# A vision tower's linear attention: half of the last softmax moved into the last round, and the order of the work after it

## The chip, the cores and the metric

The kernel runs on one core of a Trainium2 chip. The core has five engines with a queue of instructions each, which are worked off in order: TensorE (PE in the profile; its weight loads are listed as PEld), VectorE (DVE), ScalarE (ACT), GpSimd (POOL) and SyncE (SP), which here issues most of the DMA transfers. The metric is device time in microseconds. Before the change three runs took 2774.36, 2775.22 and 2785.34 us; their median is 2775.22 us.

## What is computed

A batch of 128 images goes through a tokenizer and two transformer layers. The stream `h` holds 128 images x 64 tokens x 256 features. The change lies in the attention of layer 1, and in the first steps of the routing of the layer's experts that follows:

```python
def _to_heads(y, R, C, H, hd):
    y = y.reshape(R, C, H, hd).transpose(0, 2, 1, 3)
    return jnp.transpose(y, (2, 1, 0, 3)).reshape(1, H, C, R * hd)

q = _to_heads(x @ Wq.T + bq, R, C, H, hd)      # R = 128 images, C = 64 tokens, H = 8 heads
k = _to_heads(x @ Wk.T + bk, R, C, H, hd)
v = _to_heads(x @ Wv.T + bv, R, C, H, hd)
q = jax.nn.softmax(q, axis=-1)                  # over images and head features
k = jax.nn.softmax(k, axis=-2)                  # over the tokens of a head
q = q * float(q.shape[-1]) ** 0.5
context = jnp.einsum('bhnd,bhne->bhde', k, v)
out = jnp.einsum('bhnd,bhde->hbne', q, context)
# h = h + out, and then
logits = layernorm(h) @ gate_w + gate_b         # routing: 8 experts
idx = jnp.argmax(softmax(logits), axis=-1)      # each token goes to one expert
```

The head of a row is not a slice of the features here: the reshape cuts each image's 64 x 256 block so that eight neighbouring tokens form one head. Multiplying k by q first gives a small matrix of 64 x 64 scores for a head, and its product with v gives the output.

## The kernel before

**Rounds.** `linear_attention` (L1084 to L1436) goes through four rounds `n`, each for 16 tokens, that is, for two heads ("halves" `hh` 0 and 1). In a round, step `i` of 16 projects one token: `queries_keys` (L1179) multiplies it with the weights of q and k in TensorE, and `queries_keys_kept` (L1184) adds the bias in DVE and writes the result to the buffer `qk`. Step `i` fills column block `i` of 8 of the 128 columns (`t g`), so that half 0 is whole after steps 0 to 7, and half 1 after steps 8 to 15. `prepare` (L1390) does the layer norm and transposes of the tokens that come next.

**The softmax of a round lies in the following round.** The dictionary `work`, filled by `at(n, i, ...)` (L1351), says which steps go behind the projection `i` of round `n`. For the heads of round `n` these are, in round `n + 1`:

- `largest` (L1215, DVE), `maximum` (L1225: a transpose on TensorE, a reduction and a diagonal matrix on DVE), `spread` (L1233: a matmul that broadcasts the maxima), `q_less` (L1237, DVE) and `q_exp` (L1241, ACT): the exponential of q
- `k_max` (L1246, DVE), `k_less` (L1251, POOL), `k_exp` (L1255, ACT), `k_sum` (L1259, DVE), `k_over_sum` (L1263, POOL, for the last half of the last heads DVE): the softmax of k
- `values` (L1190: TensorE, copied by ACT) in the heads' own round, and `values_transposed` (L1204: TensorE, then four ACT instructions with the bias)
- `scores` (L1270): 64 matmuls, each as two passes in the trace, that alternate between the halves; `scores_kept` and `scores_sums` (L1279, L1283) normalise them; `mixed` (L1290, TensorE) multiplies with the values, `added` (L1301, DVE) adds to the stripe of 64 features of the stream, and `written` (L1307, SP) issues the stripe's two writes, to `hx` for the experts and to `out`.

**The stripe after it.** In round `n + 2` the finished stripe is transposed (`transposed`, L1315: TensorE, copied by ACT), multiplied with the gate weights (`gates`, L1328, TensorE; `gates_added`, L1340, DVE), and its partial row statistics are taken (`moments`, L1311, DVE).

The loop runs over `range(6)`: rounds 4 and 5 have no projections. Round 4 holds the values and the whole softmax of the last heads along with the gates of the heads before, and round 5 the gates and moments of the last stripe. The order of the instructions is written out by hand (`manual_schedule`): each engine's queue follows the order of the calls.

**Buffers that tie the steps together.** Two buffers for `qk`, two for the stripe `h`, one each for `v`, `vT`, `m`, `mc`, `dg`, `ks` and `am`; PSUM pools of three (`pp`: projections, values), two (`pt`: transposes), one (`ps`: maximum, broadcast, scores) and two buffers (`po`: products, gates).

**The routing.** `route` (L1495) is called next. Its tiles take the memory that the attention's pools give back. It first makes mean and reciprocal root of each row from the partial statistics `sth` (L1518 to L1527), then transposes the gate sums `lgs` (L1533), subtracts, and scales with `rs` (L1539 to L1540).

Of the kernel before, what the change touches and what calls it, by code (L numbers as in the profile page):

```python
# [11 lines left out]
F32 = mybir.dt.float32  # L12
# [7 lines left out]
P = 128  # L20
# [1063 lines left out]
def linear_attention(c, hd, hx, out, lgs, sth, wqk, bqk, wv, bv, wgb):  # L1084
# [4 lines left out]
    tc, nc = c.tc, c.nc  # L1089
    NG = 4  # L1090
    with (
# [70 lines left out]
        class Heads:  # L1162
# [9 lines left out]
            def load(self):  # L1172
                self.h = hp.tile([P, T, 64], F32, tag="h", name="h", bufs=2)
                nc.sync.dma_start(self.h, hd[:, :, self.n * 64 : self.n * 64 + 64])
# [49 lines left out]

            def maximum(self):  # L1225
# [37 lines left out]
            def k_over_sum(self, hh, n):  # L1263
                eng = nc.vector if self.n == 3 and hh == 1 else nc.gpsimd
                x = self.k[:, 16 * n : 16 * n + 16, hh * 64 : hh * 64 + 64]
                eng.tensor_mul(x, x, bcast(self.ks[:, hh, 16 * n : 16 * n + 16], 2, 64))
# [3 lines left out]
            def scores(self):  # L1270
                self.pa = pss.tile([P, 64], F32, tag="ps", name="pa")
                for d in range(32):
                    for hh in range(2):
                        r = slice(hh * 64, hh * 64 + 64)
                        nc.tensor.matmul(
                            self.pa[r, :], self.k[:, d, r], self.q[:, d, r], start=(d == 0), stop=(d == 31)
                        )
# [73 lines left out]
        def at(n, i, f, *a):  # L1351
            work.setdefault((n, i), []).append(lambda: f(*a))

        for n, x in enumerate(heads):
# [17 lines left out]
            for k, i in enumerate((0, 0, 1, 1, 2, 3, 4, 5)):  # L1372
                at(m, i + (4 if n == 3 else 0), x.values_transposed, k)
            at(m, 10, x.scores)
            at(m, 10, x.scores_kept)
# [4 lines left out]
            at(m, 15, x.written)  # L1380

            for k in range(8):
                at(m + 1, 1 + k, x.transposed, k)
            for k in range(4):
                at(m + 1, 8 + k, x.moments, 16 * k, 16)
            for k in range(2):
                at(m + 1, 4 + 4 * k, x.gates, k)
                at(m + 1, 5 + 4 * k, x.gates_added, k)

# [15 lines left out]
        with tc.manual_schedule():  # L1405
# [11 lines left out]
            for n in range(6):  # L1417
                x = heads[n] if n < 4 else None
                if x:
                    x.begin()  # L1420
                for i in range(16):
                    if x:
                        x.queries_keys(i)
                        prepare(4 * n + i // NG, i % NG)
                        if i == 8:
                            x.load()
                    for step in work.pop((n, i), ()):
                        step()
                    if x:
                        x.queries_keys_kept(i)  # L1430
                        if n < 3 and i in (6, 7, 8, 10, 11, 12, 14, 15):
                            x.values((6, 7, 8, 10, 11, 12, 14, 15).index(i))
                    elif n == 4 and i < 4:
                        heads[3].values(2 * i)
                        heads[3].values(2 * i + 1)
# [3 lines left out]
class Routing:  # L1439


    def __init__(self, c, gp, wg, bg):
# [36 lines left out]
        nc.vector.memset(self.one, 1.0)  # L1479

# [14 lines left out]
def route(c, k, gfd):  # L1495
# [5 lines left out]
    with (  # L1501
# [12 lines left out]
        mean, rs, var, m, gf, pos = (g1(n) for n in ("mean", "rs", "var", "m", "gf", "pos"))  # L1514


        parts = k.sth.rearrange("p t n (s k) -> p t (n s) k", k=3)
        nc.vector.tensor_reduce(mean, parts[:, :, :, 1], AX.X, ALU.add)  # L1518
        nc.vector.tensor_scalar_mul(mean, mean, 1.0 / 8)
        nc.vector.tensor_sub(dev, parts[:, :, :, 1], bcast(mean, 2, 8))  # L1520
        nc.vector.tensor_mul(sq, dev, dev)
        nc.vector.tensor_reduce(m, sq, AX.X, ALU.add)
        nc.vector.tensor_reduce(var, parts[:, :, :, 2], AX.X, ALU.add)
        nc.vector.tensor_scalar(m, m, 1.0 / 8, LN_EPS, ALU.mult, ALU.add)
        nc.vector.tensor_scalar_mul(var, var, 1.0 / D)
        nc.vector.tensor_add(var, var, m)
        inverse_root(c, var, rs, m)  # L1527
# [273 lines left out]
def vit_tower(ctx: ExitStack, tc: tile.TileContext, a, out):  # L1801
# [16 lines left out]
    with tc.tile_pool(name="gate", bufs=1) as gp:  # L1818
        k = Routing(c, gp, a["wg"], a["bg"])
        linear_attention(c, hd, hx, out, k.lgs, k.sth, a["wqk1"], a["bqk1"], a["wv1"], a["bv1"], a["wg"])  # L1820
        experts(c, hx, gfd, out, a["we1"], a["we2"], a["be2"], lambda: route(c, k, gfd))
# [68 lines left out]
```

## Time and profile before

| what | us |
|---|---|
| median of three runs | 2775.22 |
| profiled execution | 2783.14 |
| its span | 2781.3 |
| PE busy in the span | 2609.6 |
| DVE busy in the span | 2036.5 |
| linear attention, first projection | 1962.9 |
| last projection kept (L1186 ends) | 2214.92 |
| scores of the last heads normalised (L1288 ends) | 2257.84 |
| last stripe added (L1305 ends) | 2271.86 |
| first statistic of the routing (L1518) starts | 2292.94 |
| `rs` first used (L1540) starts | 2301.53 |

The lower rows are moments after the start of the span, read from the timeline. A timeline line has the start, the duration, the engine, the line of the code, the operation, output and inputs, the number of instructions merged, and in brackets how long the engine had been idle and what ended that. "PEclk" or granted clock is the share of its full clock that TensorE was given. A line in the table of windows has a stretch of time and its length, and then, for PE, PEld, DVE, ACT and POOL, the busy time and the number of instructions.

### The profile page before, as it was taken

What the parts mean: (1) busy time and instruction counts of PE and PEld (TensorE: products, weight loads), DVE (VectorE), ACT (ScalarE), POOL (GpSimd) and SP (SyncE); (2) the same over time, 40 slices, a digit from 0 to 9 for tenths busy, and PEclk for the clock granted to TensorE, in tenths of its full rate; (3) what the DMA queues carried; (4) which work ended last, traced back from release to release, by engine and by line L of the source; (5) the groups of instructions that cost most, each with busy time, mean ns of one, the idle gap of its engine ahead of it and who ended that gap; (6) DMA issues with size and microseconds to landing.
All of it is one profiled execution on the core that took longest, in us unless ns stands there. A gap on an engine that the chain in (4) does not pass through costs nothing. (4 is left out here: it accounts for less than half of the span.)

```text
span 2781.3 us, 76925 instructions
## 1 busy us (share of the span) xinstructions
PE 2609.6 (94%) x33260; PEld 1748.0 (63%) x33260; DVE 2036.5 (73%) x3017; ACT 1627.1 (59%) x3411; POOL 1628.1 (59%) x1389
## 2 busy tenths in 40 slices
PE   7989999999999998899999999998899965999997
PEld 3553444444444443688888888887466645888886
DVE  6759999999998997577777777776467755444443
ACT  3228889888888887466665666565354432233332
POOL 3329888888888887765566565643133211454444
PEclk9999999999999999899999999999899975999999
DMA  3000000000000000000000000000444433555554
GB/s 107 31 12 1 2 1 2 1 2 2 1 2 1 2 2 2 12 11 18 11 18 11 11 18 11 18 11 17 115 89 109 101 90 109 173 191 190 194 194 133
DMA packets 138063, 140.80 MB, mean 51 GB/s; under 512 B 107923, under 2 KB 121509, under 8 KB 130032
## 3 DMA queue, kind: packets, MB, share of 16 engines
q1 hardware_dynamic: 126816, 117.91, 14.2%
q0 software_dynamic: 7648, 14.77, 1.7%
q8 instruction: 263, 4.31, 0.6%
q10 hardware_dynamic: 3248, 3.09, 0.4%
q14 instruction: 88, 0.72, 0.1%
HBM read 103.93 MB, written 32.54 MB: 49 GB/s over the span
## 5 line engine op out<-in xcount | busy, mean ns | idle before, releaser
L495 POOL TENSOR_TENSOR m<-q,k 128x1024 f32<-128x1024 f32 x384 | 719.0, 1903 | 30.5 <-PE sc L297 16.1
L487 DVE TENSOR_TENSOR m<-pc,k 128x2048 f32<-128x2048 f32 (+1 forms) x320 | 646.7, 2058 | 0.5 <-ACT q L431 0.5
L297 PE MATMUL sc<-m,wide 128*32 128x512 f32 x4096 | 529.6, 598 | 12.0 <-DVE m L487 7.1
L496 ACT ACTIVATE m<-m 128x1024 f32<-128x1024 f32 x384 | 402.2, 1049 | 5.9 <-POOL m L495 5.2
L297 PEld LDWEIGHTS sc<-m,wide 128*32 128x32 f32 x4096 | 126.4, 109 | 259.7 <-issue 146.2
L505 ACT ACTIVATE m<-k,q 128x64 f32<-128x64 f32 x1024 | 270.9, 339 | 0.8 <-DVE k L378 0.8
L946 DVE TENSOR_REDUCE mx<-sc 128x16 f32<-128x1024 f32 x128 | 156.1, 1220 | 154.7 <-PE sc L934 131.9
L961 POOL TENSOR_TENSOR e<-e,mx 128x1024 f32<-128x1024 f32 x128 | 243.4, 1902 | 10.1 <-POOL mx L960 0.2
L906 ACT COPY qk<-pqk 128x512 f32<-128x512 f32 x256 | 139.0, 605 | 134.3 <-PE pqk L902 134.3
L960 POOL TENSOR_TENSOR mx<-mx,gate 128x16 f32<-128x16 f32 x128 | 27.6, 216 | 316.9 <-ACT z L991 153.2
L1724 PE MATMUL ph<-xt,w1s 128*128 128x256 f32 x896 | 203.3, 386 | 3.4 <-DVE xt L1715 3.0
L1740 PE MATMUL po<-w2s,hT 128*128 128x256 f32 x896 | 198.0, 379 | 0.0
L973 ACT COPY pT<-pt 128x512 f32<-128x512 f32 x256 | 138.8, 600 | 98.9 <-PE pt L970 98.1
L1724 PEld LDWEIGHTS ph<-xt,w1s 128*128 128x128 f32 x896 | 173.3, 194 | 29.2 <-DVE xt L1715 3.8
L1740 PEld LDWEIGHTS po<-w2s,hT 128*128 128x128 f32 x896 | 168.1, 190 | 21.7
L902 PE MATMUL pqk<-xT,w 64*128 64x128 f32 x2048 | 169.5, 289 | 2.7 <-issue 2.7
L947 DVE TENSOR_TENSOR e<-sc,mx 128x1024 f32<-128x1024 f32 x128 | 156.8, 1225 | 4.4
L1728 ACT ACTIVATE hT<-ph,w1s 128x256 f32<-128x256 f32 x224 | 93.3, 470 | 106.6 <-PE ph L1724 106.6
L1758 POOL DMA_INDIRECT out<-y,rout x56 | 56.7, 1013 | 168.6 <-ACT hT L1728 125.1
L953 DVE TENSOR_REDUCE mx<-e 128x16 f32<-128x1024 f32 x128 | 153.3, 1198 | 2.5 <-ACT e L950 2.4
L902 PEld LDWEIGHTS pqk<-xT,w 64*128 64x128 f32 x2048 | 142.3, 189 | 20.4 <-issue 11.1
L970 PE MATMUL pt<-ident,e 128*128 128x128 f32 x1024 | 142.9, 280 | 5.0 <-POOL e L961 1.5
(290 smaller groups left out, 4986.7 us busy)
## 6 DMA issues: line engine op xcount, KB each, us to landing
w1s<-in_we SPq DMA_DIRECT2D x30, 1028.0 KB, 5.3
w2s<-in_we SPq DMA_DIRECT2D x30, 1024.0 KB, 5.0
hd<-h SPq DMA_DIRECT2D x16, 512.0 KB, 3.2
x<-hd SPq DMA_DIRECT2D x16, 512.0 KB, 3.9
h<-hd SPq DMA_DIRECT2D x4, 2048.0 KB, 12.7
hx<-h SPq DMA_DIRECT2D x4, 2048.0 KB, 11.4
out<-h SPq DMA_DIRECT2D x4, 2048.0 KB, 20.6
xt<-in_x SPq DMA_DIRECT2D x15, 512.0 KB, 3.5
```

Source lines behind the costliest of these rows:

```text
L297: nc.tensor.matmul(dst[j : j + 32], wide[:, hf, s : s + 32], part, start=start, stop=stop)
L487: nc.vector.tensor_tensor(m, bcast(self.pq[:, hf, i : i + n], 3, T), k, ALU.max)
L495: nc.gpsimd.tensor_tensor(m, bcast(self.q[:, hf, s : s + 2], 3, T), k, ALU.subtract)
L496: nc.scalar.activation(m, m, AF.Relu)
L505: nc.scalar.activation(self.parts[i, hf][:, q], self.blk.k[:, hf, i], AF.Relu, bias=self.q[:, hf, i - NB // 2, q : q + 1], scale=-1.0,)
L902: nc.tensor.matmul(pq[par][:, k, eh, :], w[r, f : f + P], self.xT[r, fc], start=True, stop=True)
L946: nc.vector.tensor_reduce(mx, sc, AX.X, ALU.max)
L947: nc.vector.tensor_sub(e, sc, bcast(mx, 2, T))
L953: nc.vector.tensor_reduce(self.sm[x], self.e[x], AX.X, ALU.add)
L961: nc.gpsimd.tensor_mul(e, e, bcast(sm, 2, T))
L1724: nc.tensor.matmul(ph[:, j], self.w1[:, w0 : w0 + P], self.xt[:, fc], start=(fc == 0), stop=(fc == 1))
L1740: nc.tensor.matmul(po, self.hT[:, f, r * P : r * P + P], self.w2[:, f, :], start=(f == 0), stop=(f == 7))
```

## The change

- The softmax of the last heads is split by halves. Half 0, whole after step 7 of round 3, goes into steps 9 to 15 of round 3 (`largest_of`, `maximum_of`, `spread_of`, `q_less_of`, `q_exp_of`, `k_exp_of`, and the old steps of k for half 0). Half 1 follows the last projection.
- Rounds 4 and 5 are replaced by `last`, which writes out one order: softmax of half 1 between the eight `values`; `scores` of half 0 and, after the last values and two transposes, of half 1; the sums; products and additions; the writes; and after these the transposes, gates and moments of the stripes of heads 2 and 3.
- Three of the four groups of moments of heads 1 go from round 3 to `last`, as fillings between the steps of heads 3.
- The stripe of heads 3 lies in a `qk` buffer instead of an `h` buffer, and its load is issued in step 11 of round 3.
- The row statistics go from `route` to a method `statistics` of `Routing`, called in `last`, with the attention's own tiles as scratch. `mean` and `rs` become tiles of the pool that outlives the attention.

```diff
             def load(self):
-                self.h = hp.tile([P, T, 64], F32, tag="h", name="h", bufs=2)
+                if self.n == 3:
+                    h = hp.tile([P, 2, 32, P], F32, tag="qk", name="h3", bufs=2)
+                    self.h = h[:, 0].rearrange("p d n -> p (d n)").rearrange("p (t f) -> p t f", f=64)
+                else:
+                    self.h = hp.tile([P, T, 64], F32, tag="h", name="h", bufs=2)
                 nc.sync.dma_start(self.h, hd[:, :, self.n * 64 : self.n * 64 + 64])
...
+            def largest_of(self, hh):
+                r = slice(hh * 64, hh * 64 + 64)
+                if hh == 0:
+                    self.m = hp.tile([P, 8, P], F32, tag="m", name="m")
+                m = self.m.rearrange("p s n -> p (s n)")[:, hh * 512 : hh * 512 + 512]
+                self.mh = m = m.rearrange("p (s n) -> p s n", n=64)
+                nc.vector.tensor_max(m, self.q[:, 0:8, r], self.q[:, 8:16, r])
+                for s in (16, 24):
+                    nc.vector.tensor_max(m, m, self.q[:, s : s + 8, r])
+                for s in (4, 2, 1):
+                    nc.vector.tensor_max(m[:, 0:s], m[:, 0:s], m[:, s : 2 * s])
+
+            def maximum_of(self, hh):
+                pool, tag = (pss, "ps") if hh else (pst, "pt")
+                pm = pool.tile([64, P], F32, tag=tag, name="pm")
+                nc.tensor.transpose(pm, self.mh[:, 0, :], c.ident)
+                self.mc = hp.tile([P, 1], F32, tag="mc", name="mc")
+                self.dg = hp.tile([P, P], F32, tag="dg", name="dg")
+                nc.vector.tensor_reduce(self.mc[0:64], pm, AX.X, ALU.max)
+                nc.vector.tensor_scalar_mul(self.dg[0:64, 0:64], c.ident[0:64, 0:64], self.mc[0:64])
+
+            def spread_of(self, hh):
+                pool, tag = (pss, "ps") if hh else (pst, "pt")
+                self.pb = pool.tile([P, 64], F32, tag=tag, name="pb")
+                nc.tensor.matmul(self.pb, ones[0:64], self.dg[0:64, 0:64], start=True, stop=True)
+
+            def q_less_of(self, hh, n):
+                x = self.q[:, 16 * n : 16 * n + 16, hh * 64 : hh * 64 + 64]
+                nc.vector.tensor_sub(x, x, bcast(self.pb, 1, 16))
...
-            def scores(self):
-                self.pa = pss.tile([P, 64], F32, tag="ps", name="pa")
+            def scores(self, heads=(0, 1)):
+                if 0 in heads:
+                    self.pa = pss.tile([P, 64], F32, tag="ps", name="pa")
                 for d in range(32):
-                    for hh in range(2):
+                    for hh in heads:
...
-        for n, x in enumerate(heads):
+        for n, x in enumerate(heads[:3]):
...
             at(m, 10, x.scores)
+            if m == 3:
+                at(m, 10, heads[3].k_max, 0)
             at(m, 10, x.scores_kept)
...
             at(m, 15, x.written)
+            if n == 2:
+                continue
 
             for k in range(8):
                 at(m + 1, 1 + k, x.transposed, k)
-            for k in range(4):
+            for k in range(4 if n == 0 else 1):
                 at(m + 1, 8 + k, x.moments, 16 * k, 16)
...
+        x = heads[3]
+        at(3, 9, x.largest_of, 0)
+        at(3, 11, x.load)
+        at(3, 11, x.maximum_of, 0)
+        at(3, 12, x.spread_of, 0)
+        for i in range(2):
+            at(3, 11, x.k_less, 0, i)
+            at(3, 12 + i, x.q_less_of, 0, i)
+            at(3, 13, x.k_exp_of, 0, i)
+            at(3, 14, x.q_exp_of, 0, i)
+            at(3, 15, x.k_over_sum, 0, i)
+        at(3, 14, x.k_sum, 0)
+
+        def last():
+            x, y, z = heads[3], heads[2], heads[1]
+            x.k_max(1)
+            x.values(0)
+            x.k_less(1, 0)
+            x.k_less(1, 1)
+            x.largest_of(1)
+            x.values(1)
+            x.values(2)
+            x.k_exp_of(1, 0)
+            x.maximum_of(1)
+            x.values(3)
+            x.k_exp_of(1, 1)
+            x.spread_of(1)
+            x.q_less_of(1, 0)
+            x.values(4)
+            x.q_exp_of(1, 0)
+            x.q_less_of(1, 1)
+            x.k_sum(1)
+            x.values(5)
+            x.q_exp_of(1, 1)
+            x.k_over_sum(1, 1)
+            x.k_over_sum(1, 0)
+            x.values(6)
+            x.scores((0,))
+            x.values(7)
+            z.moments(16, 16)
+            for i in range(2):
+                x.values_transposed(i)
+            x.scores((1,))
+            x.scores_kept()
+            x.values_transposed(2)
+            x.scores_sums()
+            x.values_transposed(3)
+            z.moments(32, 16)
+            for i in range(4):
+                x.mixed(i)
+                for j in (4 + 2 * i, 5 + 2 * i):
+                    if j < 8:
+                        x.values_transposed(j)
+                (z if i == 0 else y).moments((48, 0, 16, 32)[i], 16)
+                x.added(i)
+            x.written()
+            for i in range(4):
+                y.transposed(i)
+            y.gates(0)
+            x.moments(0, 64)
+            for i in range(4, 8):
+                y.transposed(i)
+            y.gates_added(0)
+            y.gates(1)
+            y.moments(48, 16)
+            for i in range(4):
+                x.transposed(i)
+            y.gates_added(1)
+            t = gp.tile([P, NG, D], F32, tag="x", name="dev", bufs=4)
+            routing.statistics(t, gp.tile([P, NG, D], F32, tag="x", name="var", bufs=4))
+            x.gates(0)
+            x.gates_added(0)
+            for i in range(4, 8):
+                x.transposed(i)
+            x.gates(1)
+            x.gates_added(1)
...
-                eng = nc.vector if self.n == 3 and hh == 1 else nc.gpsimd
+                eng = nc.vector if (self.n, hh, n) == (3, 1, 0) else nc.gpsimd
```

`statistics` has the instructions that stood at L1518 to L1527, and `route` begins with the transposes of `lgs`.

More of the change, by code (lines that the diff above doesn't have):

```diff
@@ L1081, in expert_attention, with linear_attention @@
         assert not work
-def linear_attention(c, hd, hx, out, lgs, sth, wqk, bqk, wv, bv, wgb):
+def linear_attention(c, hd, hx, out, k, wqk, bqk, wv, bv, wgb):
     tc, nc = c.tc, c.nc
+    lgs, sth, routing = k.lgs, k.sth, k
     NG = 4
@@ L1223, in largest, with q_exp_of, k_exp_of @@
                         nc.vector.tensor_max(self.m[:, 0:s], self.m[:, 0:s], self.m[:, s : 2 * s])
+            def largest_of(self, hh):
[24 more added lines that the diff above has]
+                nc.vector.tensor_sub(x, x, bcast(self.pb, 1, 16))
+            def q_exp_of(self, hh, n):
+                x = self.q[:, 16 * n : 16 * n + 16, hh * 64 : hh * 64 + 64]
+                nc.scalar.activation(x, x, AF.Exp)
+            def k_exp_of(self, hh, n):
+                x = self.k[:, 16 * n : 16 * n + 16, hh * 64 : hh * 64 + 64]
+                nc.scalar.activation(x, x, AF.Exp)
             def maximum(self):
@@ L1372, in linear_attention @@
             for k, i in enumerate((0, 0, 1, 1, 2, 3, 4, 5)):
-                at(m, i + (4 if n == 3 else 0), x.values_transposed, k)
+                at(m, i, x.values_transposed, k)
             at(m, 10, x.scores)
+            if m == 3:
+                at(m, 10, heads[3].k_max, 0)
             at(m, 10, x.scores_kept)
@@ L1416, in linear_attention @@
             groups[4].load()
[L1417 to L1420, printed above, removed]
+            for n, x in enumerate(heads):
+                x.begin()
                 for i in range(16):
[L1422 to L1426, printed above, removed]
+                    x.queries_keys(i)
+                    prepare(4 * n + i // NG, i % NG)
+                    if n < 3 and i == 8:
+                        x.load()
                     for step in work.pop((n, i), ()):
                         step()
[L1429 to L1435, printed above, removed]
+                    x.queries_keys_kept(i)
+                    if n < 3 and i in (6, 7, 8, 10, 11, 12, 14, 15):
+                        x.values((6, 7, 8, 10, 11, 12, 14, 15).index(i))
+            last()
         assert not work
@@ L1479, in __init__, with statistics @@
         nc.vector.memset(self.one, 1.0)
+        self.c = c
+        self.mean, self.rs = (gp.tile([P, T], F32, name=n) for n in ("mean", "rs"))
+    def statistics(self, t, u):
+        nc, mean = self.c.nc, self.mean
+        dev, sq = (t[:, 2 * i : 2 * i + 2].rearrange("p a (t n) -> p (a t) n", n=8) for i in range(2))
+        var, m = (u[:, i, 0:T] for i in range(2))
+        parts = self.sth.rearrange("p t n (s k) -> p t (n s) k", k=3)
+        nc.vector.tensor_reduce(mean, parts[:, :, :, 1], AX.X, ALU.add)
+        nc.vector.tensor_scalar_mul(mean, mean, 1.0 / 8)
+        nc.vector.tensor_sub(dev, parts[:, :, :, 1], bcast(mean, 2, 8))
+        nc.vector.tensor_mul(sq, dev, dev)
+        nc.vector.tensor_reduce(m, sq, AX.X, ALU.add)
+        nc.vector.tensor_reduce(var, parts[:, :, :, 2], AX.X, ALU.add)
+        nc.vector.tensor_scalar(m, m, 1.0 / 8, LN_EPS, ALU.mult, ALU.add)
+        nc.vector.tensor_scalar_mul(var, var, 1.0 / D)
+        nc.vector.tensor_add(var, var, m)
+        inverse_root(self.c, var, self.rs, m)
 def inverse_root(c, x, y, t):
@@ L1513, in route @@
         pb, oh, cs, dev, sq = g8("pb"), g8("oh"), g8("cs"), g8("dev"), g8("sq")
[L1514 to L1527, printed above, removed]
+        m, gf, pos = (g1(n) for n in ("m", "gf", "pos"))
+        mean, rs = k.mean, k.rs
         pl = gpp.tile([P, 2, 4, 4, 32], F32, name="pl")
@@ L1819, in vit_tower @@
         k = Routing(c, gp, a["wg"], a["bg"])
-        linear_attention(c, hd, hx, out, k.lgs, k.sth, a["wqk1"], a["bqk1"], a["wv1"], a["bv1"], a["wg"])
+        linear_attention(c, hd, hx, out, k, a["wqk1"], a["bqk1"], a["wv1"], a["bv1"], a["wg"])
         experts(c, hx, gfd, out, a["we1"], a["we2"], a["be2"], lambda: route(c, k, gfd))
```

## The prediction

> **What bounds the kernel now.** I read the page first: TensorE is busy for 94% of the span, but the share is lowest, and the granted clock too, in slices 32 to 34, where the linear attention ends and the routing begins. The page's chain of waits names only the last instruction, so it decides nothing here. I then asked for the windows by stage, and last for the timeline from the last round to the routing, which gives the order.
>
> The windows; columns are busy time of PE, weight loads, DVE, ACT, POOL, then granted clock, DMA share, GB/s:
>
> ```profile
> 2151.00:2215.00 64.00, 58.59 (x440) 35.99 (x439) 46.60 (x118) 30.17 (x64) 16.62 (x12) 0.97 0.43 91
> 2215.00:2257.90 42.90, 33.14 (x276) 24.42 (x274) 32.22 (x89) 24.34 (x52) 11.24 (x6) 0.88 0.41 98
> 2257.90:2293.00 35.10, 23.43 (x184) 18.75 (x184) 14.60 (x75) 4.49 (x8) 0.00 (x0) 0.67 0.50 120
> 2293.00:2318.00 25.00, 0.99 (x4) 0.92 (x4) 23.09 (x71) 0.79 (x2) 0.00 (x0) 0.50 0.06 18
> ```
>
> The first row is round 3, bound by TensorE. In the next two, 78 us after the last projection, no engine is full: a chain runs through all of them. The timeline of that chain:
>
> ```profile
> 2190.92 3.95 PE L1275 MATMUL pa<-qk 128*64 128x64 f32 x128
> 2194.92 0.22 DVE L1281 COPY am<-pa 128x64 f32<-128x64 f32 x1 [2.89 <-PE pa L1275]
> ...
> 2198.74 2.00 PE L1297 MATMUL po<-am,vT 64*128 64x64 f32 x32 [0.91 <-DVE am L1288]
> ...
> 2200.77 1.28 DVE L1305 TENSOR_TENSOR h<-h,po 128x512 f32<-128x512 f32 x2 [1.49 <-PE po L1297]
> ...
> 2214.23 0.69 DVE L1186 TENSOR_TENSOR qk<-pq,bs 128x512 f32<-128x512 f32 x1 [0.64 <-PE pq L1182]
> ...
> 2257.61 0.23 DVE L1288 TENSOR_TENSOR am<-am,rq 128x64 f32<-128x64 f32 x1
> 2257.89 12.47 PEld L1297 LDWEIGHTS po<-am,vT 64*128 64x128 f32 x128 [2.45 <-DVE am L1288]
> 2257.89 12.66 PE L1297 MATMUL po<-am,vT 64*128 64x64 f32 x128 [2.31 <-DVE am L1288]
> ...
> 2270.57 1.29 DVE L1305 TENSOR_TENSOR h<-h,po 128x512 f32<-128x512 f32 x2 [2.13 <-PE po L1297]
> 2271.89 0.51 SPq L1309 DMA_DIRECT2D hx<-h  x1
> 2272.44 9.07 SPq L1309 DMA_DIRECT2D out<-h  x1
> ...
> 2292.94 0.83 DVE L1518 TENSOR_REDUCE mean<-sth 128x64 f32<-128x512 f32 x1 [6.00 <-DMA out<-h]
> ...
> 2301.53 0.69 DVE L1540 TENSOR_TENSOR pb<-pb,rs 128x512 f32<-128x512 f32 x1
> ```
>
> The reader is to see four stretches: last projection kept at 2214.92; 42.9 us of softmax until the scores are normalised (2257.84); 14.0 us of products and additions until 2271.86; 29.7 us until 2301.53. The last holds gates, moments and a DVE idle for 6.00 us on the write of the stream, which lands 21.0 us after its first issue, and only then the row statistics. From L1540 on the code is the same in both kernels.
>
> The granted clock in the third stretch:
>
> ```profile
> 2176.00:2180.00 4.00, 0.41 (x4) 0.17 (x2) 1.59 (x4) 4.00 (x4) 2.89 (x2) 1.00 0.00 0
> 2180.00:2184.00 4.00, 3.58 (x11) 2.17 (x12) 3.96 (x11) 2.91 (x5) 2.16 (x2) 0.60 0.02 4
> ...
> 2260.00:2264.00 4.00, 4.00 (x42) 4.00 (x40) 1.54 (x3) 0.00 (x0) 0.00 (x0) 0.50 0.02 4
> 2264.00:2268.00 4.00, 4.00 (x42) 4.00 (x40) 1.87 (x4) 0.00 (x0) 0.00 (x0) 0.50 0.00 0
> ```
>
> An idle of about 4 us costs the clock, and the 64-column products at full occupation don't bring it back: they take 12.66/4 = 3.17 us per quarter, against 2.00 us at 2198.74.
>
> **The change part by part.** I carry the new order forward on all queues with these durations and compare the same four points.
>
> *Round 3.* DVE loses three groups of moments (3 x 2.11 = 6.3 us) and gains the half maximum (3 x 0.69 + 0.43 + 0.29 + 0.2 = 3.0), a k maximum (2.27), a reduction and a diagonal (0.58), two subtractions (2 x 1.21), a sum and a reciprocal (2.64): 10.9 us. Not the sum but the waits count. Half maximum and k maximum fit where moments stood and where DVE idled for 2.89 us before L1281. But the transpose of the maximum stands on TensorE behind the first product (ends 2200.7), and DVE waits for it with the next kept projection and the additions queued behind: transpose 0.3, reduction and diagonal 0.6, kept projection 0.7, addition done 2203.7 instead of 2202.05. The next product starts on the addition's first half and ends 2205.1; the broadcast queued behind it (0.4) is what the first subtraction awaits: subtraction to 2206.7, kept projection 2207.4, addition 2208.7; product 2 to 2210.7; second subtraction and kept projection fit in that time; addition 2212.1, sum and reciprocal 2214.7, kept projection 2215.4, addition 2216.7, last kept projection 2217.4: **2.5 us later** than 2214.92. ACT (four exponentials of half an operand, about 1.05 each) and POOL (four multiplications or subtractions of 1.90) idle there: L1199 was preceded by 17.6 idle us on ACT, L1253 by 38.6 on POOL. The load of the last feature stripe now waits only for the scores of head pair 2 (2194.9; it was issued at 2197.83), ahead of that pair's writes on SP; it lands after some 12.7 us, over 30 us before use. Both cost nothing.
>
> *Softmax and scores.* DVE from 2217.4: k maximum 2.3, half maximum 3.1, to 2222.8; transpose, reduction, diagonal to 2223.8. TensorE does values 0 to 2 meanwhile, then value 3 (3.62/2 = 1.8 plus a small gap, 1.86) and the broadcast, to 2225.4. From there TensorE is the longest: values 4 to 6 to 2231.0. Beside it DVE subtracts twice, sums, inverts (2230.5) and multiplies one half while POOL takes the other (2232.4). Then scores of half 0, value 7 (1.86) and its copy (0.6), two transposes (1.1), scores of half 1, copy, sum matmul, reciprocal and product (1.7).
>
> The scores were 128 passes in 3.95 us, 31 ns each, the halves alternating between two column ranges. A projection pass streams 512 columns in about 0.43 us, 54 ns for 64, so neighbouring passes overlap. Split, nothing alternates. Bounds for 64 passes: 31 ns, 2.0 us; 30 ns weight load plus 54 ns stream with no overlap, 5.4 us. I take 54 ns, 3.5 us, since consecutive passes of the same range (the projections) overlap their weight loads.
>
> So: 2231.0 + 3.5 + 1.86 + 0.6 + 1.1 + 3.5 + 1.7 = 2243.3, **14.5 us earlier** than 2257.84.
>
> The Trainium skill, "TensorE: Matmul & The Clock Gate", Part 3, says that a weight load overlaps matmuls in flight only where the row group differs. Split halves use all rows, so by that rule alone each half would take the 5.4 us, and the gain below shrinks by 3.8 us; the trace before, whose halves also share all rows, shows 3.81 us of weight loads inside 3.95 us of passes, against it.
>
> *Products and additions.* Four value transposes moved in between make TensorE 4 x 3.17 + 4 x 1.07 = 17.0 us at the low clock, while DVE has five groups of moments and four additions, 5 x 2.1 + 4 x 1.3 = 15.7; that is the bound at full clock. From the normalised scores to the last addition I take 17.3 (the low clock arriving after the first product), bounds 15.7 and 18.8: 2260.6, **11.3 us earlier**.
>
> The same page, Part 1, has the full clock return after some 3.4 us of activity; the rows at 2260 to 2268 show 0.50 over fully busy windows and differ. By the page this stretch would be at 15.7 us and the gain 1.6 us more.
>
> *After the last addition.* DVE in order: moments of the stripe 64 x 0.13 = 8.3, gate addition 0.69, moments 2.1, gate addition 0.69, statistics 8.3 (the same instructions that stood between 2292.94 and 2301.53, now without the subtractions between them), two gate additions 1.4, product 0.7, eight subtractions with the wait for the last transpose 1.6: 23.8 us, to 2284.4. TensorE and ACT do sixteen stripe transposes and four gate matmuls beside it: 2277.43 to 2281.74 shows 4.3 us per quarter, 17.2 us and some start at the low clock; they end about 2281, with the statistics. The write lands at 2260.6 + 21.0 = 2281.6, the first product of the routing asks for it at 2282.1. Three things end within 1 us, so each earlier one is worthless, each later one costs.
>
> Sum: 2284.4 against 2301.53, **17.1 us less**. The routing and experts (from 2301.53 to the end) stay. The profiled execution took 2783.14 us (span 2781.3); it would take 2766.0. That execution lies 7.9 us above the median of the runs, 2775.22 (2774.36, 2775.22, 2785.34); from the median the forecast is 2758 us.
>
> **The rivals.**
> 1. Dear scores and an early low clock: split passes without overlap, and the clock falls at the first scores (about 2236) instead of in the products. For it: low-activity products didn't bring the clock back. Against: the scores at 2190.92 kept 1.00. At 84 ns a pass, 3.8 us are lost; with values, transposes and scores at the low clock some 5 more: gain 7 to 11 us, 2764 to 2768.
> 2. The write takes over: the wait that the page shows (6.00 us) stays, as the stripe's write now runs beside other DMA or is issued later. Against: the write rows agree (20.4 median, 21.0 most). Every microsecond beyond 0.5 counts; 5 us more gives 2763.
> 3. Slower: the waits added to round 3 let the clock fall there. One gap of over 3.5 us on TensorE between 2198 and 2217 does it, as at 2176. Then five steps of projection and product take 6.9 us instead of 3.85 (15 us), eight values 3.6 instead of 1.86 (14 us), scores 3: 32 us lost, 15 slower, 2790. Against: the largest gap that I find there is 1.4 us. It decides only from a gap of 3.5 us.
> 4. Cheap scores (2.0 each) and the full clock throughout: 17.1 + 3.0 + 1.6, gain near 21 us, 2754.
>
> **How the numbers follow.** Forecast 0.57, rival 1 0.20, rival 2 0.08, rival 3 0.06, rival 4 0.09. The likeliest case is 2758 with 2754 to 2763. The range takes rivals 1, 2 and 4, with some 3 us of scatter between runs: 2750 to 2771. A 0.5% step, 14 us, is about what these runs can tell from no change; it lies at 2761.3, inside the forecast's own range. Faster: most of the forecast (0.50) and rival 4 (0.09), a little of rival 2: 0.61. Slower: rival 3, 0.06. The rest is 0.33.
>
> **What would show it.** Right: last kept projection 2 to 3 us later than before relative to the round's start; half scores of 3 to 4 us each; normalised scores 26 us after the last kept projection (before: 42.9); last addition to the routing's first product about 21.5 us, with hardly a wait for the write. Wrong: a granted clock below 1.0 in round 3, a half score of 2.0 or 5.4 us, DVE idle on the write for several microseconds, or a routing and expert stage that itself changes its length.

## The result and the profile after

The changed kernel takes 2760.72 us (median of five runs, 2759.70 to 2765.45), the kernel before, run beside it, 2777.53 us. The ratio is 0.9931 with a 95% interval of 0.9917 to 0.9944: it is faster by 0.7%. Later comparisons of the unchanged pair gave 0.9931 (0.9914 to 0.9948) and 0.9947 (0.9926 to 0.9968). The profiled execution took 2759.7 us, its span is 2757.9 us.

Executions of both kernels fall into two groups some 8 us apart, which part in the tokenizer, long before the change (its last convolution matmul starts at 125 to 126 us or at 131 to 133 us), and the two profiles that are compared here belong to different groups; so stages are measured from the first projection of the linear attention.

The time by stage, in us. "Rounds" runs from the first projection to the last kept one, "softmax" to the normalised scores, "products" to the last addition, "after" to the first use of `rs`; "experts" goes from the end of the routing's last matmul to the end of the span:

| execution | rounds | softmax | products | after | sum of these | experts |
|---|---|---|---|---|---|---|
| before | 251.98 | 42.92 | 14.02 | 29.67 | 338.59 | 435.44 |
| after | 256.44 | 31.13 | 14.91 | 23.41 | 325.89 | 433.42 |
| after, forecast | 254.5 | 25.9 | 17.3 | 23.8 | 321.5 | 435.4 |

So the linear attention gives 12.7 us where 17.1 were forecast, and the experts, untouched, some 2 us more. The windows of the changed kernel by stage, with smaller windows where the clock matters (time, then busy time of PE, weight loads, DVE, ACT, POOL, then granted clock, DMA share, GB/s):

```profile
2141.30:2210.70 69.40, 63.12 (x446) 38.31 (x446) 51.11 (x84) 34.90 (x69) 24.16 (x16) 0.93 0.41 86
2210.70:2241.80 31.10, 25.84 (x210) 21.83 (x208) 18.06 (x34) 11.68 (x24) 7.46 (x3) 0.95 0.56 135
2241.80:2256.70 14.90, 14.60 (x176) 12.23 (x176) 14.90 (x89) 7.83 (x26) 0.00 (x0) 1.00 0.01 2
2256.70:2280.10 23.40, 12.28 (x75) 6.80 (x72) 21.87 (x117) 6.34 (x12) 0.00 (x0) 0.87 0.74 180
...
2192.00:2196.00 4.00, 4.00 (x20) 1.78 (x18) 2.22 (x5) 0.00 (x0) 0.00 (x0) 0.57 1.37 220
...
2204.00:2208.00 4.00, 4.00 (x36) 2.24 (x34) 2.79 (x3) 0.00 (x0) 1.60 (x1) 0.79 0.00 0
...
2216.00:2220.00 4.00, 0.70 (x3) 0.61 (x4) 3.41 (x5) 0.70 (x1) 1.66 (x1) 0.92 0.91 214
2220.00:2224.00 4.00, 4.00 (x13) 2.89 (x12) 0.85 (x3) 0.95 (x2) 0.00 (x0) 0.65 0.90 219
```

Three things are to be seen. The products stage, whose windows stood at 0.50 before, holds the full clock, and DVE is busy in all of it. The clock is lost earlier instead: in round 3 (0.57 and 0.79), and once in the softmax (0.65), behind a window in which TensorE worked for 0.70 us of 4. The timeline of the same stretches:

```profile
2189.63 2.00 PE L1344 MATMUL po<-am,vT 64*128 64x64 f32 x32 [0.91 <-DVE am L1335]
2191.57 0.30 PE L1248 MATMUL pm<-ident,m 128*64 128x128 f32 x1
2191.70 3.27 PE L1189 MATMUL pq<-w,xT 128*128 128x512 f32 x4
...
2202.57 3.52 PE L1189 MATMUL pq<-w,xT 128*128 128x512 f32 x4
...
2213.07 4.59 POOL L1299 TENSOR_TENSOR qk<-qk,ks 128x1024 f32<-128x1024 f32 x2 [2.91 <-DVE ks L1295]
...
2213.62 4.58 DVE L1241 TENSOR_TENSOR m<-m,qk 128x512 f32<-128x512 f32 x2
...
2219.30 0.40 PE L1248 MATMUL pm<-ident,m 128*64 128x128 f32 x1 [4.18 <-DVE m L1243]
...
2219.50 3.52 PE L1203 MATMUL pv<-wvs,xT 128*128 128x256 f32 x8
...
2222.94 0.43 PE L1257 MATMUL pb<-dg,ones 64*128 64x64 f32 x2
...
2228.68 3.94 PE L1322 MATMUL pa<-qk 128*64 128x64 f32 x64
...
2236.25 3.94 PE L1322 MATMUL pa<-qk 128*64 128x64 f32 x64
...
2256.73 0.51 SPq L1356 DMA_DIRECT2D hx<-h  x1
...
2277.99 0.69 DVE L1664 TENSOR_TENSOR dev<-wsum,mean 128x512 f32<-128x512 f32 x1 [0.57 <-DMA out<-h]
...
2280.12 0.69 DVE L1670 TENSOR_TENSOR pb<-pb,rs 128x512 f32<-128x512 f32 x1
```

A projection of four passes takes 3.27 and 3.52 us instead of 1.98. Two steps of the half maximum (L1241) take 4.58 us, 2.29 each, beside POOL's subtractions, which take as long. TensorE idles for 4.18 us before the transpose of the maximum, and the value behind it takes 3.52 us instead of 1.9. A half of the scores takes 3.94 us. The wait on the stream's write is 0.57 us, where it was 6.00.

### The profile page after: what moved, and what is told of

Read it like the earlier page. It is cut to its first block, busy times and chain, and to the rows that moved or that the text cites. A ratio compares the mean times of both kernels' runs of the same rounds, so it can differ in the third digit from the quotient of the medians.

```text
span 2757.9 us, 76947 instructions
## 1 busy us (share of the span) xinstructions
PE 2602.5 (94%) x33263; PEld 1744.7 (63%) x33263; DVE 2038.5 (74%) x3024; ACT 1628.9 (59%) x3415; POOL 1633.7 (59%) x1390
## 6 DMA issues: line engine op xcount, KB each, us to landing
h<-hd SPq DMA_DIRECT2D x4, 2048.0 KB, 12.8
out<-h SPq DMA_DIRECT2D x4, 2048.0 KB, 21.3
```

## The experiments

The theory: the gain of the softmax and of the stage after the last addition is real; the part that is missing is lost to a clash of DVE and POOL early in the softmax, to the clock that falls behind it, to the split of the scores, and in round 3 to added waits and clock falls. The rivals: the scatter between executions makes the difference; or the write, the place of the moments, or TensorE's order sets the end instead.

**The changed kernel again**, without an edit.

> The changed kernel once more, as the yardstick for the runs beside it. Between the first projection and the first use of rs the two profiles differ by 325.9 against 338.6 us, 12.7 us; the rest of the 23.4 us between the two spans lies before the attention (8.7) and in the experts (2.0). Theory A: only the 12.7 us, and perhaps 2 in the experts, belong to the change, and the 8.7 are scatter between executions: the median is then 2760 to 2766, and the first projection of this profile lies anywhere from 1954 to 1963. Theory B: the change also makes the stages ahead of it faster: the first projection lies at 1954 to 1955 again, and the median at 2757 to 2761.

Measured: 2760.05 us in the median (six runs), ratio 0.9931. The first projection comes at 1961.0 us, as it does before the change (1962.9), and the stages repeat: 255.85, 31.07, 14.90, 23.38, with 433.73 us of experts. Its span is 2764.2 us, 17.1 below that of before in the same group; the two profiles shown above differ by 23.4, of which 8.7 lie ahead of the attention. The scatter doesn't make the gain.

**The kernel before again.**

> The kernel before, unchanged, profiled a second time. Theory A (what the change does after the first projection is the same in every execution): linear attention from the first projection to the first use of the reciprocal root takes 338 to 339 us, with 64.6 us for round 3, 42.9 for the softmax and 29.6 after the last addition, whether the first projection comes at 1954 or at 1962 us. Routing's end to the end of the span takes 435.4 us again if the 1.7 to 2.0 us that the experts are shorter after the change belong to the change, and 433 to 434 if they are scatter. Theory B (the readings of before belong to its slower tokenizer): with a first projection at 1954 us the linear attention itself is several microseconds different.

Measured: 341.25 us for the linear attention (rounds 252.89, softmax 43.41, products 15.29, after 29.66), experts 434.96. The stages repeat within 1.3 us, and the experts stay at 435. Round 3 is 66.2 us instead of 64.6, and the timeline of this execution tells why:

```profile
2198.67 2.00 PE L1297 MATMUL po<-am,vT 64*128 64x64 f32 x32 [0.91 <-DVE am L1288]
2200.60 3.42 PE L1182 MATMUL pq<-w,xT 128*128 128x512 f32 x4
```

The clock falls once (0.70 in the window from 2202 us) in the kernel before too, with none of the new waits. The longest idle of TensorE nearby is 0.91 us, which the first execution of before has as well, without a fall. So a fall in round 3 is not brought by the change alone.

The first profile of before, against which 12.7 us were counted, had no such fall. Over the two profiles of before (338.59 and 341.25 us) and the three of the changed kernel (325.89, 325.20 and, in the last run below, 324.44) the linear attention gives 14.7 us on average and the experts 1.8. Together that is 16.6 us, about what the medians show (16.8).

**Statistics back in the routing.**

```diff
-            t = gp.tile([P, NG, D], F32, tag="x", name="dev", bufs=4)
-            routing.statistics(t, gp.tile([P, NG, D], F32, tag="x", name="var", bufs=4))
 ...
+        k.statistics(gp.tile([P, 4, D], F32, name="t"), gp.tile([P, 4, D], F32, name="u"))
```

> Mean, variance and reciprocal root of the rows are computed in the routing again, with scratch tiles there; the rest of the new order stays. Theory: the write of the last stripe lands some 21.3 us after the last addition, and in the changed kernel the statistics (8.1 us) fill that time. Put back, all but the first sum and its scaling wait for the write: from the last addition to the first use of rs 28 to 30 us instead of 23.4, with DVE idle for about 6 us on the write, and the time 5 to 6 us above the changed kernel. Rival: the wait is not for the write but for gates and transposes on TensorE, which end at about the same time: then DVE waits for TensorE, and the loss is the 8 us of the statistics in full or below 2 us.

Measured: 28.79 us from the last addition, 5.4 more; ratio 0.9966 (0.9952 to 0.9980). The wait is back, at the scratch tile of the statistics:

```profile
2287.86 0.83 DVE L1612 TENSOR_TENSOR t<-sth,mean 128x512 f32<-128x512 f32 x1 [5.52 <-DMA out<-h]
```

The column in brackets is the idle time and what ended it. The statistics under the write are worth 5.4 of the 6.3 us that this stage gained. The experts take 435.53 us here, as before the change; in the eleven profiles with the statistics in the attention they take 432.8 to 434.0. The traces show where that time lies: in the first two products of the experts, the same 32 passes each in both kernels (the first two rows are of before, the last two of after):

```profile
2355.63 10.16 PE L1724 MATMUL ph<-xt,w1s 128*128 128x256 f32 x32 [0.78 <-DVE xt L1715]
...
2375.32 8.86 PE L1724 MATMUL ph<-xt,w1s 128*128 128x256 f32 x32 [2.19 <-DVE xt L1715]
...
2334.19 9.45 PE L1854 MATMUL ph<-xt,w1s 128*128 128x256 f32 x32 [0.78 <-DVE xt L1845]
...
2353.32 7.17 PE L1854 MATMUL ph<-xt,w1s 128*128 128x256 f32 x32 [2.34 <-DVE xt L1845]
```

The granted clock over the second product is 0.81 before and 1.00 after. It takes 8.7 to 8.9 us in the three profiles with the statistics in the routing and 7.17 in the eleven others. So the experts do no less work; TensorE's clock falls once less there. It comes back from its low state 5.9 to 6.1 us behind the start of the first product in those three profiles, and 3.9 to 5.6 in the others, at a point of a grid that the account of round 3 below describes. Whether the place of the statistics sets this, or chance, is not shown.

**Half 0 not inside round 3.** All steps of half 0 go behind the last projection, ahead of or between those of half 1.

```diff
-        at(3, 9, x.largest_of, 0)
-        at(3, 11, x.maximum_of, 0)
 ...
         def last():
             x, y, z = heads[3], heads[2], heads[1]
-            x.k_max(1)
+            x.largest_of(0)
+            x.k_max(0)
             x.values(0)
+            x.maximum_of(0)
+            x.k_less(0, 0)
+            x.k_less(0, 1)
+            x.k_max(1)
 ...
```

> Both halves of the last softmax come after the last projection; nothing of it is in round 3. The rest of the new order stays. Theory: round 3 returns to its old length of 64.6 us (changed kernel 69.3), and DVE's 10.9 us of half 0 stand on the path behind it, beside values that need TensorE for 15 us anyway: softmax 36 to 41 us instead of 31.1, in all 1 to 5 us slower than the changed kernel. Rival 1: half 0 is worth its full 10.9 us, and the time rises by 6 us or more. Rival 2: the half inside gains nothing, as round 3 pays as much as the tail saves: within 1 us, or faster.

Measured: softmax 43.94 us (12.8 more), round 3 64.8 (4.6 less), the sum 335.47; ratio 0.9991 (0.9976 to 1.0005), no gain left that these runs can tell. The theory that put half 0 at 1 to 5 us fell: DVE and POOL can't do both halves beside the values, TensorE waits for both maxima and both diagonals, and its clock goes with them (0.50 from 2227.7 to 2241.4 us):

```profile
2229.74 0.42 PE L1248 MATMUL pm<-ident,m 128*64 128x128 f32 x1 [6.10 <-DVE m L1243]
...
2236.67 0.69 PE L1257 MATMUL pb<-dg,ones 64*128 64x64 f32 x2 [3.10 <-DVE dg L1252]
```

**The maximum first.** `largest_of(1)` goes ahead of `k_max(1)`, so POOL's subtractions, which need the k maximum, start later.

```diff
+            x.largest_of(1)
             x.k_max(1)
             x.values(0)
             x.k_less(1, 0)
             x.k_less(1, 1)
-            x.largest_of(1)
```

> After the last projection DVE makes the maximum over q of half 1 first and the maximum over k second, so that POOL's subtractions start when DVE's tensor-by-tensor maxima are done. Theory: POOL's subtractions stretched two of DVE's maxima from 0.69 to 2.29 us each and that let TensorE idle and the clock fall; in this order the two take 0.69 us, TensorE doesn't idle for 4 us, value 3 takes 1.9 us instead of 3.5, and normalised scores come about 5 us earlier (26 us after the last kept projection). Rival 1: the long maxima have another cause, such as the columns 64 to 127 that they read: they stay at 2.29 us and the gain is below 1 us. Rival 2: the clash moves to another pair of instructions, and 2 us or less are gained.

Measured: softmax 27.32 us, 3.8 less; ratio 0.9930 (0.9911 to 0.9949), not to be told from the changed kernel's, so the gain rests on the trace. The timeline of this kernel:

```profile
2203.51 1.88 PE L1189 MATMUL pq<-w,xT 128*128 128x512 f32 x4
...
2221.58 1.42 DVE L1241 TENSOR_TENSOR m<-m,qk 128x512 f32<-128x512 f32 x2
...
2226.32 3.76 POOL L1299 TENSOR_TENSOR qk<-qk,ks 128x1024 f32<-128x1024 f32 x2 [5.32 <-DVE ks L1295]
...
2226.47 1.80 DVE L1252 TENSOR_SCALAR dg<-ident,mc 64x64 f32<-64x64 f32 x1
...
2228.32 0.43 PE L1257 MATMUL pb<-dg,ones 64*128 64x64 f32 x2 [2.17 <-DVE dg L1252]
```

The two steps are at 0.71 us each again. But the clash has moved: the diagonal matrix takes 1.80 us instead of 0.25. It starts 0.15 us after POOL's first subtraction and ends when that one (half of 3.76 us) ends, and TensorE waits 2.17 us for it. The half maximum's first step (L1239) is held up too: it takes 1.65 us instead of 0.68, beside POOL's last multiplication of half 0. The first line belongs to round 3, whose code is the same here as in the changed kernel: the projection behind the maximum's transpose took 1.88 us, not 3.27, and the round 67.0 us, not 69.4.

**POOL's subtractions on DVE.** A direct test of the clash: the order stays, only the engine changes.

```diff
             def k_less(self, hh, n):
-                nc.gpsimd.tensor_sub(x, x, ...)
+                eng = nc.vector if (self.n, hh) == (3, 1) else nc.gpsimd
+                eng.tensor_sub(x, x, ...)
```

> The two subtractions of the k maximum of half 1 go from POOL to DVE; nothing else is changed. Theory A (DVE and POOL block each other): without POOL's two instructions the second and third step of the half maximum take 0.69 us each again instead of 2.29, POOL takes no time there, and DVE, which now does 2 x 1.22 = 2.4 us more itself, has its diagonal matrix some 0.8 us earlier after the last kept projection than the 9.6 us of the changed kernel; the softmax takes 30 to 31 us (31.13 before this edit). Theory B (the two steps are long for another reason, as their place behind the k maximum or their operands): they stay at 2.29 us, the 2.4 us of subtractions come on top, and the softmax takes about 33.5 us.

Measured: softmax 30.28 us, 0.8 less, though DVE does two more large instructions:

```profile
2222.44 2.36 DVE L1300 TENSOR_TENSOR qk<-qk,ks 128x1024 f32<-128x1024 f32 x2
...
2225.43 1.42 DVE L1241 TENSOR_TENSOR m<-m,qk 128x512 f32<-128x512 f32 x2
...
2227.95 0.30 PE L1248 MATMUL pm<-ident,m 128*64 128x128 f32 x1 [3.42 <-DVE m L1243]
```

Theory A held: with POOL silent the steps take 0.71 us in the same place, on the same operands. The numbers of the changed kernel fit two engines that exclude each other for whole instructions. DVE's first step (L1239) ends at 2213.59, POOL's first subtraction at 2215.35, DVE's second step at 2215.90, POOL's second subtraction at 2217.66, DVE's third step at 2218.20. So they end in turn, POOL 1.76 us behind DVE and DVE 0.55 us behind POOL, each a little less than it takes alone (1.90 and 0.69).

The Trainium skill, "SBUF — State Buffer", "SBUF: two separate sides", says the same: VectorE and GpSimd share one pair of ports as an exclusive lock, against a VectorE instruction with two SBUF inputs or in a two-port mode, and the one that comes second "fully blocks". These traces agree, with 2.29 us against 0.69 and 1.80 against 0.25.

**Scores together.** Half 0's scores go back to half 1's.

```diff
             x.values(6)
-            x.scores((0,))
             x.values(7)
 ...
-            x.scores((1,))
+            x.scores()
```

> The scores of both halves are computed together again, alternating, at the place where those of half 1 stand. Theory: TensorE sets the end of the softmax, so the half that stood between values 6 and 7 (3.94 us) leaves the path, and 128 alternating passes take 3.95 us as before the change: normalised scores about 27.2 us after the last kept projection instead of 31.1, time 3.9 us below the changed kernel. Rival: the first half is hidden, since the second half waits for the exponentials and the division of half 1 anyway: no change within 1 us.

Measured: softmax 26.98 us, 4.1 less; ratio 0.9934 (0.9915 to 0.9953), again not to be told from the changed kernel's. The 128 alternating passes take what 64 of one half take:

```profile
2232.43 3.95 PE L1322 MATMUL pa<-qk 128*64 128x64 f32 x128
```

**The early broadcast.** The maximum's transpose goes ahead of the scores of head pair 2 and the broadcast ahead of the first product, so that no kept projection, addition or subtraction queues behind them.

```diff
+            if m == 3:
+                at(m, 10, heads[3].maximum_of, 0)
 ...
+            if m == 3:
+                at(m, 11, heads[3].spread_of, 0)
 ...
-        at(3, 11, x.maximum_of, 0)
-        at(3, 12, x.spread_of, 0)
```

> In round 3 the transpose of half 0's maxima stands ahead of the scores of heads 2 and the broadcast ahead of the first product, instead of behind products 0 and 1. Theory: the 4.5 us by which round 3 became longer come from DVE's waits for these two matmuls, with the projections and additions queued behind, and from the lower clock that follows; in this order the last projection is kept about 252.5 to 253.5 us after the first projection of the attention (before the change 252.0, after it 256.4), the projections of steps 12 and 14 take 2.0 us instead of 3.3 and 3.5, and the time falls by 3 to 4 us. Rival: the 4.6 us more DVE work in round 3 set its length: it stays at 255 us or more and the time moves by less than 1 us.

Measured: round 3 takes 67.1 us, 2.3 less than in the changed kernel's profile and 2.5 more than in the first profile of before; ratio 0.9940 (0.9921 to 0.9959), not to be told from the changed kernel. The additions run as before the change, without the waits on the broadcast, but 0.34 us is now waited for the transpose ahead of the scores, and one projection takes 3.68 us: one fall of the clock is left. In the last run of this edit, with the two others (below), no fall came and round 3 took 65.1 us, 0.5 more than before: so the edit takes off 1.9 of the 2.4 us of waits, which is too little to be timed beside the falls.

**Gates early.** The transposes and gates of head pair 2 go back into the softmax, behind the first scores; their sums stand ahead of the products.

```diff
             x.scores((0,))
             x.values(7)
             z.moments(16, 16)
+            for i in range(4):
+                y.transposed(i)
+            y.gates(0)
+            for i in range(4, 8):
+                y.transposed(i)
+            y.gates(1)
 ...
+            y.gates_added_both()
             for i in range(4):
                 x.mixed(i)
 ...
```

> The eight transposes and two gate matmuls of the stripe of heads 2 stand again ahead of the last scores (between the last values and the value transposes), and their additions between the sums and the products; the rest stays. Theory: TensorE sets the end of the softmax, so their 8.6 us come on the path: softmax 39 to 40 us instead of 31.1; after the last addition DVE has 1.4 us less and the write lands at 21.3, so 21.5 to 22.5 us instead of 23.4: 6 to 8 us slower. Rival: they fit into waits of TensorE, and less than 2 us are lost.

Measured: softmax 38.46 us (7.3 more), products 16.10 (1.2 more), and 23.55 after the last addition, where 23.41 stood; ratio 0.9986 (0.9970 to 1.0001). TensorE is the end of the softmax from the broadcast on, so all its work there is paid in full; behind the last addition the write keeps the time (DVE waits 2.01 us for it), so nothing comes back:

```profile
2287.57 0.69 DVE L1669 TENSOR_TENSOR dev<-wsum,mean 128x512 f32<-128x512 f32 x1 [2.01 <-DMA out<-h]
```

Here lies the other large part of the gain: the stream's transposes and gates went under the statistics and the write.

**All three edits** (maximum first, scores together, early broadcast).

> Scores together, the q maximum of half 1 first, and the broadcast of half 0 early in round 3, all three. Theory: scores and the clash lie one after the other on the same chain, so the softmax falls from 31.1 to 23 to 24 us after the last kept projection, and round 3 is 67 us or a little less instead of 69.3; from the first projection to the first use of rs 314 to 317 us instead of 325 to 326, and the time 8 to 11 us below the changed kernel, near 2751. Rival: with TensorE relieved of 8 us the chain over DVE, POOL and ACT (maximum, subtraction, exponential, sum, division) becomes the longest, and the two gains don't add: softmax 26 to 27 us, 5 us in all.

Measured: softmax 23.44 us, which is 7.7 less than the changed kernel's, where the single edits gave 3.8 and 4.1; the sum 317.00; 2758.58 us, ratio 0.9923 (0.9903 to 0.9942). To set it against the changed kernel, both ran again side by side.

> The version with the early broadcast, the half maximum first and the scores together, again, beside the changed kernel on the same chip. Theory A (the stages add up to the time): from the first projection to the first use of the reciprocal root 317 us, 8 to 9 us less than the changed kernel's 325 to 326, so a ratio to before about 0.003 lower than the changed kernel's. Theory B (what is won there is lost in later stages or in scatter): the same 317 us, but a ratio within 0.001 of the changed kernel's.

> The changed kernel without an edit, for the comparison with the version above: 325 to 326 us from the first projection to the first use of the reciprocal root, ratio to before 0.993.

Measured: 315.15 against 324.44 us for the linear attention (softmax 25.13 here, with one fall of the clock in it, against 30.86); 2757.61 us (2752.90 to 2763.93) against 2765.68 (2761.75 to 2769.48), ratios to before 0.9923 (0.9900 to 0.9946) and 0.9947 (0.9926 to 0.9968). The stages add up to the time: 9.3 us in the trace, 8.1 in the medians. The intervals of the two ratios overlap, so the step from the changed kernel to this one rests on the stages; this is the fastest version that ran. No run tested the place of the moments by itself.

## Why the prediction was right, and where its steps were not

The sign, the size (16.8 us less in the medians, 17.2 forecast from the median) and the forecast of 2758 us against 2760.72 hold. That the number came so near is in part luck. Of the four stages two were right and two wrong, with errors of both signs; over all profiles the linear attention gave 14.7 us where 17.1 were forecast, and the experts, forecast to stay, gave another 1.8. Of the signs that the prediction named for being right, the half scores (3.94 us) and the 21.3 us from the last addition to the routing's first product came, the normalised scores 26 us after the last kept projection did not (31.1); and two of its signs for being wrong came, a clock below 1.0 in round 3 and an expert stage of another length.

*Round 3, "2.5 us later".* The waits were sized right. Where round 3 kept the full clock (the run with the maximum first, whose round 3 is unchanged code) it took 67.0 us against 64.6, 2.4 more. In the profile after it took 69.4, because the clock fell twice. This is the mechanism of rival 3, "the waits added to round 3 let the clock fall there". The step that failed is its threshold, "it decides only from a gap of 3.5 us": the falls came behind idles of 0.91 and of 0.69 and 0.19 us. They were also far shorter than rival 3 had it: one or two projections at half clock, 2.4 us, not 32. Whether the clock falls differs between executions of the same code: in eight profiles of this round 3, five had two falls (69.4 us) and three had none (67.0); in the two profiles of before one had one. The traces show what parts them. In all fourteen the granted clock is 1.00 or 0.50, and it changes only at points of a grid, 3.41 us apart. The changed kernel (first two rows) and the run with the maximum first (last two), in the steps of the grid around the first product (the third number from the end is the granted clock):

```profile
2188.65:2192.06 3.41, 2.50 (x35) 2.20 (x35) 0.94 (x3) 2.48 (x4) 0.13 (x1) 1.00 1.34 232
2192.06:2195.47 3.41, 3.41 (x10) 1.25 (x8) 2.16 (x5) 0.00 (x0) 0.00 (x0) 0.50 1.36 220
...
2200.69:2204.10 3.41, 2.66 (x35) 2.36 (x36) 1.02 (x4) 2.25 (x3) 0.00 (x0) 1.00 1.33 227
2204.10:2207.51 3.41, 2.99 (x29) 1.84 (x28) 1.96 (x4) 0.00 (x0) 0.00 (x0) 1.00 1.36 220
```

In the five profiles with falls a point of the grid lies 2.22 to 2.42 us behind the start of the first product, in the three without 2.65 to 2.67; in those of before it is 2.34 with the fall and 2.55 without. So the same code keeps or loses the clock by where the grid happens to lie.

*Softmax and scores, "14.5 us earlier" from 25.9 us of softmax.* It took 31.13, 5.2 more, and the scores are the small part. Of the steps: the maximum's transpose was to start 5.4 us behind the last kept projection and started at 8.6; the broadcast was to end at 8.0 and ended at 12.7. These 4.7 us have one cause and its effect. "Half maximum 3.1" was taken from rows where POOL was silent, and the clash with POOL made it 6.3; TensorE then idled 4.18 us where some 1 us was reckoned with, and value 3 ran at the low clock, 3.52 us instead of 1.86. The scores add 0.9 (the rest of the stage was 0.4 shorter): 3.94 us a half, where 3.5 was taken between bounds of 2.0 and 5.4. At 61.6 ns a pass neighbours of one column range do overlap their weight loads, and the 84 ns that the Trainium skill's rule on row groups ("TensorE: Matmul & The Clock Gate", Part 3) would make of it did not come.

*Products, 17.3 us.* They took 14.91. The term that failed is "the low clock arriving after the first product": the clock stayed at 1.00, and DVE set the time, as the lower bound of 15.7 said, which itself was 0.8 too long. The reading behind that term, that 64-column products lose the clock, went too far: before, they began at 0.50 and didn't raise it; here they began at 1.00 and kept it. What the forecast worked out from the same page, Part 1, 15.7 us, came nearer.

*After the last addition, 23.8 us.* It took 23.41. The write landed 21.2 us after its issue (21.0 forecast) and DVE waited 0.57 us for it, where it was to be ready 0.5 us ahead. The experiment with the statistics in the routing shows the coupling: without them under the write 5.4 us come back, so rival 2's "every microsecond beyond 0.5 counts" was true of the place, and its 5 us did not come.

*"The routing and experts stay."* The routing did (44.3 us); the experts became 1.8 us shorter on average, together with the move of the statistics: their first two products ran at a higher clock (above), and whether the move brought that is open.

*The rivals.* Rival 1 foresaw a gain of only 7 to 11 us by dear scores and an early low clock. The low clock did come early, in the softmax and ahead of the scores, but by the clash, not by the split passes; scores and products then ran at 1.00. Rival 4's full clock came from value 4 to the last addition, without its cheap scores. In sum, against before: rounds -4.5, softmax 11.8, products -0.9, after 6.3, together 12.7; the forecast had -2.5, 17.0, -3.3 and 5.9. (These are the two profiles of the table; the mean of all is 14.7.)

## What to carry to other kernels

When steps are put beside each other on DVE and POOL, read whether the rows from which their durations come had the other engine silent: here 3.2 us of a clash cost 4.7 on the path, since TensorE's idle took its clock along. A split of interleaved work (here the two halves of the scores, 3.95 us together and 3.94 each alone) is only worth its place if something else waited for the first part. And where a long transfer has to land before the next stage, the cheapest cover is work of that stage that doesn't need it: the statistics under the write gave 5.4 us with no instruction removed.

## What had not been expected of the hardware

- The granted clock of TensorE fell to 0.50 for 3.41 us at a time behind idles of less than 1 us (the 0.57 to 0.79 above are means over windows of 4 us), in some executions and not in others of the same code, in the kernel before too. In these traces it changes only on a grid of 3.41 us, and a shift of the code against that grid by some 0.2 us decided whether it fell in round 3. The Trainium skill, "TensorE: Matmul & The Clock Gate", "Why this matters for your kernels", advises against idle gaps over about 3 us; these rows show falls with none of that length in the 15 us ahead of them.
- DVE and POOL exclude each other by whole instructions also where the DVE instruction is small: the 64 x 64 diagonal took 1.80 us instead of 0.25 behind a POOL subtraction. Instructions that read PSUM were not held up: the subtractions of the broadcast (L1261), the first of the two in the run with the maximum first, took 1.22 us beside POOL's second subtraction, and 1.22 beside a silent POOL in the changed kernel.
- A group of 64 score passes of one column range takes as long as 128 that alternate between two (3.94 and 3.95 us), so 61.6 against 30.9 ns a pass.
